# A projection in seven products of quarters, and work of VectorE handed to ScalarE, in a two-layer attention kernel

## The chip, the cores and the metric

The kernel runs on one core of a Trainium2 chip. The metric is device time in microseconds (us). Before the change three runs gave 2559.35, 2559.91 and 2560.78 us; their median, 2559.91 us, is the time that the change is measured against. One further execution, taken by the hardware profiler, gives the durations below; it took 2559.32 us.

Short names: PE is TensorE, and PEld its loading of weights; DVE is VectorE; ACT is ScalarE; POOL is GpSimd; SP is the engine that issues most transfers.

## The reference

The input x is 8 images of 512 channels by 32 x 32 points, so 1024 tokens. Two attention layers follow each other; all is float32.

```
# layer 0, for each of 8 images; 8 heads of 64 channels
h   = group_norm(x)
qkv = qkv_w @ h + qkv_b
q, k, v = fake_quant(q), fake_quant(k), fake_quant(v)    # 255 levels over the whole tensor
w   = softmax((q*s)^T (k*s));   a = w applied to v
x   = x + proj_w @ a + proj_b                            # "the projection"
# layer 1: one head of 512 channels
h   = group_norm(x)
q, k, v = wq h, wk h, wv h
x   = x + wp @ (softmax(q k^T / sqrt(512)) v)
```

`fake_quant` rounds x/scale, adds a zero point, clips to 0..255 and scales back. Its scale needs the minimum and the maximum over all images, so layer 0's q, k and v are computed for all images before its attention starts.

## The kernel before, in words

**Two phases.** Phase one computes layer 0's q, k and v of all images and stores them in HBM. Phase two interleaves, on all engines, the attention of layer 0 for image b+1 with layer 1 of image b, and ends with layer 1 of the last image alone.

**Attention of layer 0** (`attention`, L1018) is a generator. Its unit is one pair of heads, 512 query tokens and 128 keys; there are 512 units, and one `advance()` runs four. A unit takes: `scores` (two PE matmuls `st` into a PSUM pair, and ACT's exponential `pt<-st`); `split`, which writes `pt` as two float16 parts, the first by a cast on ACT or POOL (`two<-pt`), the second by a subtraction on DVE (`two<-pt,two`, a "sum" in the code, 128 x 1024); `over_keys` (PE matmuls `av`, which need both parts); and `totals` (PE matmuls `sm`). There are four `pt` buffers: the exponential of unit u needs the subtraction of unit u-4 (`need`, L1048). There are two PSUM pairs for `st`. In a dense step the scores of units u+6 and u+7 come first; in a late step, the one after a projection, `over_keys` of two units comes first, then the scores, then `over_keys` of the other two.

**Quantizing.** `load_pair` (L961) fetches the next pair's q, k and v; for each, `quant` (L890: times 1/scale, plus a magic number that rounds) works in place on 128 x 1024, and `quant2` (L893) clips and converts. Both are on DVE: 12 of each per image.

**Layer 1's big products** go by `seven` (L1393): a 512 x 512 product is cut into quarters and made from seven products of quarters instead of eight, with sums of quarters prepared on DVE. Two PSUM banks take turns, so product i+2 waits until product i has been read out. **The projection** (`project`, L1296) is plain: for each half of the tokens and each of four blocks of output channels, four matmuls 128 x 512; DVE then adds bias and residual in one instruction (`h<-pj,vec,h`), stores the result, and takes statistics (`gst_b<-h`) for layer 1's norm. The projection of image b+1 stands inside layer 1 of image b, in `o_run` after its fourth product (`first`, L1764): an attention step, half 0, an attention step (dense), half 1, an attention step (late), and the rest of `o_run`, into which the norm's steps (`norm1`, L1344) are placed. `norm1` normalizes the first half of the tokens at once (four DVE instructions 128 x 512) and leaves the second half as chores.

**What sets the order.** Each engine executes in program order. That order is written by a planner (`InOrder`, L72) with three clocks, `pe.t`, `dve.t` and `act.t`. A matmul moves `pe.t` by 1.677 ns per column of float32 (L213); DVE work on n elements costs `elements(n)`. `do` places work now. `later` puts work among an engine's chores with a time when its inputs are ready and a due time. Before each `do`, `fill` takes chores that fit into the gap, earliest start first, then earliest due. `settle(name)` places all chores of that name now, and `need` does so for subtractions.

```python
return 0.21 + n * 0.957e-3                 # elements(n), L159
ready = pe.t + 0.25 if ready is None else ready          # do
self.fill(ready)
self.t = max(self.t, ready) + cost
if begin + cost > limit + 0.15:            # fill, L138: does not fit, stays a chore
    continue
```

The names used below: `wp` is the projection's weights, `x_d` the HBM copy of its result, `h` (in the code `xts[b]`) the tile with the residual and then the normed input, `ao` layer 0's attention output, `gps_b` the two small matmuls of the norm, `g` the first product of layer 1.

Of the kernel before, what the change touches and what calls it, by code (L numbers as in the profile page):

```python
# [9 lines left out]
F32 = mybir.dt.float32  # L10
# [48 lines left out]
def attn_pair_kernel(  # L59
# [166 lines left out]


    def norm_steps(
        src, dst, wcol, bank, nm, ccs=range(CC), fine=False, put=None, mv=None, apply=None
    ):  # L230

        n, c0 = len(ccs), ccs[0]
        put = put or (lambda hf, cost, work: work())
        if mv is None:
            st, mv = stat_tiles(n, nm)
            for i, cc in enumerate(ccs):
                for hf in range(NH):
                    dve.bn_stats(st[:, i, hf, :], src(cc, hf))  # L240
                aggregate(mv, st, i)
                if fine and i + 1 < n:
                    yield
        yield
        ps = bank(f"gps_{nm}")[:, 0:n]
        mm(ps, lhsT=gavg, rhs=mv[:, :, 0], start=True, stop=True)

        d = small.tile([P, n], F32, tag=f"gd{n}", name=f"gd_{nm}")
        mean = small.tile([P, n], F32, tag=f"gmean{n}", name=f"gmean_{nm}")

        def offsets():
            dve.tensor_sub(d, mv[:, :, 0], ps)
            dve.tensor_copy(mean, ps)
            dve.tensor_mul(d, d, d)
            dve.tensor_add(d, d, mv[:, :, 1])

        dve.do(0.6, offsets)
        yield
        ps2 = bank(f"gps2_{nm}")[:, 0:n]
        mm(ps2, lhsT=gavg, rhs=d, start=True, stop=True)  # L260
        rstd = small.tile([P, n], F32, tag=f"grstd{n}", name=f"grstd_{nm}")
        dve.do(0.15, lambda: dve.tensor_scalar(rstd, ps2, EPS, None, ALU.add))
        nc.gpsimd.tensor_tensor(rstd, rstd, mhalf[:, 0:n], ALU.pow)
        dve.do(
            0.15, lambda: dve.tensor_mul(rstd, rstd, vec[:, wcol + c0 : wcol + c0 + n]), dve.t + 1.4
        )
        if apply is not None:
            off = small.tile([P, n], F32, tag=f"goff{n}", name=f"goff_{nm}")
            dve.scalar_tensor_tensor(off, mean, -1.0, rstd, ALU.mult, ALU.mult)
            for i, cc in enumerate(ccs):  # L270
                apply(cc, rstd[:, i : i + 1], off[:, i : i + 1])
                yield
            return
        for hf in range(NH):
            for i, cc in enumerate(ccs):
                put(hf, 0.5, lambda i=i, cc=cc, hf=hf: dve.tensor_scalar(
                    dst(cc, hf), src(cc, hf), mean[:, i : i + 1], rstd[:, i : i + 1],
                    ALU.subtract, ALU.mult,
                ))
                if fine and i % 2 == 1:  # L280
                    yield
        if not fine:
            yield
# [23 lines left out]
    with ExitStack() as fast:  # L307
# [579 lines left out]

        kept_u = l2p.tile([P, 3, 2, 256], F32, name="kept_u")

        def quant(raw, dst, i):  # L890
            dve.tensor_scalar(raw, raw, rcp[:, i : i + 1], MAGIC, ALU.mult, ALU.add)

        def quant2(raw, dst, i):  # L893
            dve.tensor_scalar(dst, raw, bhi[:, i : i + 1], MAGIC, ALU.min, ALU.subtract)
# [66 lines left out]
        def load_pair(b, j, u=None):  # L961

            nm = f"{b}_{j}"
            raws = []

            def fetch(i, src):
                if (b, j, i) == (0, 0, 2):
                    raw = aop.tile([P, NH, 512], F32, tag="ao", name="raw_first").rearrange(
                        "p h n -> p (h n)"
                    )  # L970
                else:
                    raw = raw_p.tile([P, T], F32, tag="raw", name=f"raw_{nm}_{i}")
                nc.sync.dma_start(
                    raw if i < 2 else raw.rearrange("p (t d) -> p t d", t=NT), src
                )
                raws.append(raw)

            def whole(raw, _, i):
                quant2(raw.rearrange("p (t d) -> p t d", t=NT)[:, 3::4, :], vfs[j], i)

            fetch(0, q_d[b][j])
            fetch(1, k_d[b][j])
            qt = qkp.tile([P, T], BF, tag="q", name=f"q_{nm}")
            kt = qkp.tile([P, T], BF, tag="k", name=f"k_{nm}")
            vt = qkp.tile([P, NT, P], F16, tag="v", name=f"v_{nm}")
            todo = (qt, kt, vt.rearrange("p t d -> p (t d)"))

            if b == 0:
                vfs[j] = xp.tile([P, 2, 256], F32, tag="x", name=f"vf_{nm}")[:, :, 0:P]

            def quants(i):
                for n, step in enumerate((quant, quant2, *([whole] if i == 2 and b == 0 else []))):
                    name, work = "qk" if i < 2 else "qv", lambda step=step: step(raws[i], todo[i], i)
                    if u is None or InOrder.planned:
                        dve.later(name, 0.7, work, pe.t + 12.0, 45.0)
                    else:
                        at = u + (7, 9, 15)[i] + n + (8 if b and j else 0)
                        dealt.append((at, name, work))
                        if (i, n) == (0, 1):
                            dealt.append((at, "qk", fetch_v))  # L1000

            def fetch_v():
                if len(raws) == 2:
                    fetch(2, v_d[b][:, :, bass.ts(j, P)])
                quants(2)

            if (b, j) == (0, 0):
                fetch(2, v_d[b][:, :, bass.ts(j, P)])
            quants(0)
            quants(1)  # L1010
            if u is None or InOrder.planned:
                dve.later("qk", 0.0, fetch_v)
            return qt, kt, vt
# [4 lines left out]
        def attention():  # L1018
# [138 lines left out]
            def finish(b, j, hf, u):  # L1157
# [26 lines left out]

                def divide():
                    dve.scalar_tensor_tensor(aot, aot, scl[:, 2:3], rs, ALU.mult, ALU.mult)

                def spread():
                    r = rcs[:, n * 16 : (n + 1) * 16]
# [74 lines left out]
                dma(xts[b][:, :, bass.ts(hf, 512)], x_v[b, :, :, bass.ts(hf, 512)])  # L1264

        def load_wp(b, dma):
            wps[b] = l2p.tile([P, CC, C], F32, tag="sums", name=f"wp0_{b}")
            dma(wps[b], w_sq[WP0])

        def load_first(u):  # L1270

# [21 lines left out]
            for t, src in zip(wm_tiles(b), wm_d):  # L1293
                act.dma_start(t, src)

        def project(b, bank=bank):  # L1296

            settle("ao")  # L1300
            st, mvs[b] = stat_tiles(CC, f"b{b}")
            wp0 = wps.pop(b)
            for hf in range(NH):
# [40 lines left out]
        def norm1(b, bank=bank):  # L1344
# [3 lines left out]

            def put(hf, cost, work):
                if hf == 0:  # L1350
                    dve.do(cost, work)
                else:
                    dve.later("h", cost, work, within=27.0)

            def put_sum(hf, i, work):
                if hf == 0:
                    dve.later("t4" if i == 3 else "t", elements(512), work, within=10.0 + 2.0 * i)
                else:
                    put(hf, elements(512), work)

            for n, _ in enumerate(norm_steps(
                at, at, V_GN1W, bank, f"b{b}", put=put, mv=mvs[b]
            )):
                if n == 2:
                    sums[b] = l2p.tile(
                        [P, 3, NH, CC // 2, 256], F32, tag="sums", name=f"sums2_{b}"
                    )
# [22 lines left out]
            dve.later("o", 0.25, spread, pe.t + 4.0, 5.0)  # L1390
            return rs

        def seven(nm, pairs, keep, whole, add, bank=bank):  # L1393

            nonlocal turn
            turn ^= 1  # L1400
            x, y = (bank(f"{nm}_{i}").rearrange("p (t n) -> p t n", t=2) for i in range(2))

            def product(n, ps, start):
                left, right = pairs[n]
                k = left.shape[1]
                for t in range(2):
                    for i in range(k):
                        mm(
                            ps[:, t, :], lhsT=left[:, i, bass.ts(t, P)], rhs=right[:, i, :],
                            start=start and t == 0 and i == 0, stop=(i == k - 1),  # L1410
                            skip_group_check=True,
                        )
# [4 lines left out]
                (5, x, False, whole, None),  # L1417
            )
            for i, (n, ps, start, out, m) in enumerate(work):
                awaits(free[(i + turn) % 2])  # L1420
                product(n, ps, start)
                free[(i + turn) % 2] = out(ps) if m is None else out(m, ps)
                yield i + 1

        free = [0.0, 0.0]
        turn = 0

        def slots(gq):
# [226 lines left out]
        def layer1(b, steps):  # L1655
# [46 lines left out]
            for hf in range(NH):  # L1702
# [52 lines left out]
                if last and b + 1 < B:  # L1755
                    load_wp(b + 1, act.dma_start)
                    load_x2(b + 1, act.dma_start)
                if done >= B:
                    load_x1(b, hf, 0, 1, rx, aop)
                settle("v")  # L1760
                between = [lambda: iter((1,)), lambda: iter(()), lambda: iter(())]
                if b + 1 < B and last:

                    def first():  # L1764
                        nonlocal ahead
                        yield -1
                        yield from project(b + 1, score_bank)
                        yield 2
                        ahead = norm1(b + 1, score_bank)
                        next(ahead)  # L1770
# [534 lines left out]
```

## Time and profile before

| what | us |
|---|---|
| median of three runs | 2559.91 |
| the profiled execution, by the device | 2559.32 |
| its span, first to last instruction | 2557.2 |
| from one image to the next in phase two (the same instruction, 907.76 and 1148.06) | 240.3 |
| PE idle in 940 to 1180, by the profile | 1.2 |

How to read the lines. A group's row has the line, engine, operation, output<-inputs, shapes and count, then busy time and mean duration in ns, then the idle time in front. L91 is the planner's own helper, so groups are told apart by tiles. A float32 matmul leaves two records, so half of image b's projection (16 matmuls) shows as 32. The ends of PE records are modelled; the step from start to start is what PE really takes. A timeline row has start, duration, engine, what it does, how many merged instructions, and in brackets the idle time before and what ended it.

### The profile page before, as it was taken

How to read it: one execution, taken by the hardware profiler on the slowest of the kernel's cores; microseconds unless marked ns; L12 is line 12 of the kernel's file. 1: busy time of each engine (PE TensorE's matmuls, PEld its weight loads, DVE VectorE, ACT ScalarE, POOL GpSimd, SP SyncE). 2: the span in 40 equal slices, each digit the busy share in tenths (PEclk: the TensorE clock that was granted, in tenths of full speed). 3: DMA queues.
4: the chain of work that ended last, by engine and by line, in shares of the span. 5: the costliest groups of instructions: out<-in, count | busy, mean ns of one | idle time of the engine just before them, and what ended most of it. 6: DMA issues, size and time to landing. Idle time of an engine off the chain costs nothing.

```text
span 2557.2 us, 38727 instructions
## 1 busy us (share of the span) xinstructions
PE 2515.9 (98%) x15670; PEld 1746.2 (68%) x15670; DVE 1897.6 (74%) x2747; ACT 1346.5 (53%) x1685; POOL 186.0 (7%) x167
## 2 busy tenths in 40 slices
PE   8999999999999999999999999999999999999998
PEld 4788888873357756775777577667756775777787
DVE  7887776668887778777877787777778777885544
ACT  3332223319857655665666466656655665664121
POOL 0000000001100001000100100010101000100000
PEclk9999999999999999999999999999999999999999
DMA  4533333236622232223313222322232123212211
GB/s 168 177 142 125 131 124 122 109 131 162 162 88 63 79 116 85 58 74 122 98 57 100 92 79 78 110 92 63 79 112 88 55 71 128 96 42 80 87 38 39
DMA packets 160717, 250.70 MB, mean 98 GB/s; under 512 B 27152, under 2 KB 93712, under 8 KB 159120
## 3 DMA queue, kind: packets, MB, share of 16 engines
q1 hardware_dynamic: 125792, 182.81, 21.6%
q10 hardware_dynamic: 30560, 57.71, 6.5%
q0 software_dynamic: 4176, 7.60, 1.7%
q8 instruction: 125, 2.05, 0.3%
q14 instruction: 64, 0.52, 0.1%
HBM read 153.64 MB, written 86.28 MB: 94 GB/s over the span
## 4 chain that ended last, share of the span: by engine, by line
PE 85%; DVE 5%; ACT 2%; issue 1%; DMA 1%; POOL 0%; SPq 0%; ACTq 0%; DVEq 0%
PE s L209 15%; PE o L209 13%; PE qkps L209 12%; PE pj L209 8%; PE av L209 8%; PE v2ps L209 7%; PE vps L209 6%; PE g L209 6%; PE st L209 4%; PE sm L209 3%; DVE two L91 2%; ACT pt L91 1%; PE fold L209 1%; DVE h L91 1%; DVE acc L91 0%
## 5 line engine op out<-in xcount | busy, mean ns | idle before, releaser
L91 ACT ACTIVATE pt<-st,esc 128x1024 f32<-128x1024 f32 x467 | 496.4, 1114 | 332.1 <-PE st L209 317.6
L91 DVE TENSOR_TENSOR two<-pt,two 128x1024 f16<-128x1024 f32 x467 | 561.5, 1216 | 131.0 <-POOL two L1092 100.7
L91 ACT CAST two<-pt 128x1024 f16<-128x1024 f32 x346 | 350.8, 1055 | 6.9 <-ACT p L91 5.1
L1092 POOL CAST two<-pt 128x1024 f16<-128x1024 f32 x112 | 146.0, 1304 | 1409.4 <-PE sm L209 746.3
L209 PE MATMUL av<-two,v 128*32 128x512 f16 x3968 | 245.9, 381 | 2.5 <-DVE two L91 2.1
L209 PE MATMUL s<-g,h 128*128 128x256 f32 x1024 | 233.4, 380 | 0.0
L209 PE MATMUL pj<-ao,wp 128*128 128x512 f32 x512 | 224.1, 595 | 0.6 <-DVE h L91 0.6
L209 PEld LDWEIGHTS s<-g,h 128*128 128x128 f32 x1024 | 192.9, 190 | 31.0 <-issue 4.3
L91 ACT ACTIVATE u_ring<-qkps,qkbt 128x512 f32<-128x512 f32 x89 | 60.9, 685 | 243.8 <-PE qkps L209 219.3
L209 PEld LDWEIGHTS <-v 128*32 128x32 f16 x3968 | 91.8, 96 | 140.0 <-issue 66.7
L209 PEld LDWEIGHTS pj<-ao,wp 128*128 128x128 f32 x512 | 96.0, 190 | 122.5 <-issue 110.8
L209 PE MATMUL s<-g,sums 128*128 128x256 f32 x768 | 178.4, 381 | 0.2 <-DVE p L91 0.2
L209 PE MATMUL o<-p,v 128*128 128x256 f32 x768 | 175.2, 382 | 1.0 <-DVE p L91 1.0
L209 PE MATMUL st<-q,k 64*128 64x512 bf16 x1024 | 163.4, 382 | 11.9 <-ACT pt L91 7.5
L209 PEld LDWEIGHTS o<-p,v 128*128 128x128 f32 x768 | 144.3, 190 | 27.1 <-issue 5.7
L209 PEld LDWEIGHTS s<-g,sums 128*128 128x128 f32 x768 | 144.7, 190 | 24.2 <-issue 4.6
L209 PE MATMUL sm<-two,ones 128*32 128x512 f16 x1984 | 136.0, 379 | 0.0
L209 PEld LDWEIGHTS <-k 64*128 64x128 bf16 x1024 | 34.8, 94 | 143.8 <-issue 142.2
L209 PE MATMUL qkps<-half,w_high 128*128 128x512 f32 x480 | 132.4, 398 | 0.0
L209 PE MATMUL qkps<-half,w_mix 128*128 128x512 f32 x480 | 130.6, 394 | 1.0 <-DVE half L91 1.0
L209 PE MATMUL qkps<-half,w_low 128*128 128x512 f32 x480 | 130.5, 394 | 0.0
L209 PE MATMUL v2ps<-wm,h 128*128 128x256 f32 x512 | 119.9, 383 | 1.9 <-ACT g L91 1.3
(226 smaller groups left out, 3902.2 us busy)
## 6 DMA issues: line engine op xcount, KB each, us to landing
rs<-rs_d SPq DMA_DIRECT2D x76, 256.0 KB
x<-in_x_dram SPq DMA_DIRECT2D x32, 512.0 KB
q_d<-wa SPq DMA_DIRECT2D x32, 512.0 KB
k_d<-wa SPq DMA_DIRECT2D x32, 512.0 KB
v_d<-v_ring SPq DMA_DIRECT2D x32, 512.0 KB
raw<-q_d SPq DMA_DIRECT2D x32, 512.0 KB
raw<-k_d SPq DMA_DIRECT2D x32, 512.0 KB
x_d<-h SPq DMA_DIRECT2D x64, 256.0 KB
```

The costliest lines, as they stand in the source:

```text
L91: ins = self.latest = op(*args, **kw).ins
L209: ins = nc.tensor.matmul(ps, lhsT=lhsT, rhs=rhs, **kw).ins
L1092: copy(two[:, 0], pt)
```

## The change

1. **The projection of images 1 to 7** (`project_seven`, new) goes by `seven`. Image 0 keeps the plain form and prepares the sums of the weights' quarters once (`combine_wp`), which go to HBM; `load_wp` then loads 1.5 MB per image in three transfers, where it loaded 1 MB in one, and a fourth weight sum (256 KB) is fetched at the start of each projection.
2. Its read-outs are all on DVE and add into the residual in place: seven per half, 128 x 512. Sums of quarters of `ao` are made on DVE: two 128 x 512 beforehand (`first_sums`), two at the start (`second`), and in each half four 128 x 256 between the first products. The two PSUM banks are the halves of one PSUM pair. Statistics follow after the sixth and seventh product of a half, two at each.
3. **The bias** is added to the residual by ACT, four 128 x 1024 chores per image (`add_bias`), settled when the projection starts.
4. **The norm** of layer 1 is applied by ACT instead of DVE, eight 128 x 512 per image (`scaled`); one small DVE instruction is added for the offset.
5. **Quantizing's first step**, wherever the planner's clocks are on (the later images), goes to ACT (`shift`); the second, on DVE, first settles the first.

```diff
+        if scaled:
+            off = small.tile([P, n], F32, tag=f"goff{n}", name=f"goff_{nm}")
+            dve.do(0.15, lambda: dve.scalar_tensor_tensor(
+                off, mean, -1.0, rstd, ALU.mult, ALU.mult
+            ))
...
+                if scaled:
+                    put(hf, 0.6, lambda i=i, cc=cc, hf=hf: act.activation(
+                        dst(cc, hf), src(cc, hf), AF.Identity, bias=off[:, i : i + 1],
+                        scale=rstd[:, i : i + 1],
+                    ))
...
+        def shift(raw, dst, i):
+            act.activation(raw, raw, AF.Identity, bias=magic, scale=rcp[:, i : i + 1])
...
-                    if u is None or InOrder.planned:
-                        dve.later(name, 0.7, work, pe.t + 12.0, 45.0)
+                    if InOrder.planned and n == 0:
+                        act.later(name, 1.02, lambda: shift(raws[i], todo[i], i), pe.t + 12.0, 35.0)
+                    elif u is None or InOrder.planned:
+
+                        def rest(work=work):
+                            if InOrder.planned:
+                                act.settle(name)
+                            work()
+
+                        dve.later(name, 0.7, rest, pe.t + 13.2, 45.0)
...
+                    if b and j == 1:
+                        first_sums(b)
...
-            wps[b] = l2p.tile([P, CC, C], F32, tag="sums", name=f"wp0_{b}")
-            dma(wps[b], w_sq[WP0])
+            wps[b] = w = l2p.tile([P, 6, CC // 2, C // 2], F32, tag="sums", name=f"wp0_{b}")
+            dma(w[:, 0:2].rearrange("p i k n -> p (i k) n"), w_sq[WP0][:, :, 0 : C // 2])
+            dma(w[:, 2], w_sq[WP0][:, CC // 2 :, C // 2 :])
+            dma(w[:, 3:6], wp_d[:, 0:3])
...
+        def add_bias(b):
+            for cc in range(CC):
+                act.later("xb", 1.05, lambda cc=cc: act.activation(
+                    xts[b][:, cc, :], xts[b][:, cc, :], AF.Identity,
+                    bias=vec[:, V_PB0 + cc : V_PB0 + cc + 1],
+                ), pe.t + 17.0, 24.0)
...
+        def project_seven(b, room):
+
+            settle("at")
             settle("ao")
+            act.settle("xb")
...
+            act.dma_start(s4, wp_d[:, 3])
...
+            for k in range(2):
+                dve.do(elements(512), lambda k=k: second(k))
...
+                def into(q, row, col, full, hf=hf):
+
+                    def add(ps):
+                        there = dve.do(elements(512), lambda: tt(q, ps, q, ALU.add))
+                        if full is not None:
+                            nc.sync.dma_start(x1_d[b][row][hf][:, :, col * 256 : (col + 1) * 256], q)
+                        return there
...
+                for step in seven(
+                    f"pj_{b}_{hf}",
+                    ((a11, h11), (a12, h21), (s2, th), (s3, h11), (s1, t1), (s4, h22), (a22, h21)),
+                    lambda n, ps: keeps[n](ps), into(q12, 0, 1, 1), lambda n, ps: adds[n](ps),
+                    lambda _: next(banks), True,
+                ):
+                    if step in (1, 2):
+                        for k in range(2):
+                            h = (h11, h21)[step - 1][k]
+                            args = (h, th[k], h) if step == 1 else (h, h, th[k])
+                            dve.do(elements(256), lambda args=args: tt(*args, ALU.subtract))
+                    for oc in {6: (2, 3), 7: (0, 1)}.get(step, ()):
+                        dve.later("pj", 0.62 + 0.2 * hf, lambda oc=oc, stats=stats: stats(oc), within=4.0)
+                    chore()
+                if hf + 1 < NH:
+                    yield -1
+            settle("pj")
...
             def put(hf, cost, work):
                 if hf == 0:
-                    dve.do(cost, work)
+                    act.do(cost, work, dve.t + 0.1)
                 else:
-                    dve.later("h", cost, work, within=27.0)
+                    act.later("h", cost, work, within=22.0)
...
-                        yield from project(b + 1, score_bank)
+                        yield from project(b + 1, vt)
```

More of the change, by code (lines that the diff above doesn't have):

```diff
@@ L228, in norm_steps @@
     def norm_steps(
-        src, dst, wcol, bank, nm, ccs=range(CC), fine=False, put=None, mv=None, apply=None
+        src, dst, wcol, bank, nm, ccs=range(CC), fine=False, put=None, mv=None, apply=None,
+        scaled=False,
     ):
@@ L273, in norm_steps @@
             return
+        if scaled:
[3 more added lines that the diff above has]
+            ))
         for hf in range(NH):
             for i, cc in enumerate(ccs):
[L276 to L279, printed above, removed]
+                if scaled:
[3 more added lines that the diff above has]
+                    ))
+                else:
+                    put(hf, 0.5, lambda i=i, cc=cc, hf=hf: dve.tensor_scalar(
+                        dst(cc, hf), src(cc, hf), mean[:, i : i + 1], rstd[:, i : i + 1],
+                        ALU.subtract, ALU.mult,
+                    ))
                 if fine and i % 2 == 1:
@@ L888, in attn_pair_kernel @@
         kept_u = l2p.tile([P, 3, 2, 256], F32, name="kept_u")
+        magic = const.tile([P, 1], F32, name="magic")
+        dve.memset(magic, MAGIC)
         def quant(raw, dst, i):
             dve.tensor_scalar(raw, raw, rcp[:, i : i + 1], MAGIC, ALU.mult, ALU.add)
+        def shift(raw, dst, i):
+            act.activation(raw, raw, AF.Identity, bias=magic, scale=rcp[:, i : i + 1])
         def quant2(raw, dst, i):
@@ L1294, in load_wm, with combine_wp @@
                 act.dma_start(t, src)
-        def project(b, bank=bank):
-            settle("ao")
+        wp_d = dram.tile([P, 4, CC // 2, C // 2], F32, tag="wp", name="wp_d")
+        def combine_wp():
+            wc = l2p.tile([P, 3, NT // 2, 256], F32, tag="vsum", name="wp_combined").rearrange(
+                "p a (s k) n -> p (a s) k n", k=2
+            )
+            a11, a12, a21, a22 = (
+                wps[0][:, k * CC // 2 : (k + 1) * CC // 2, m * 256 : (m + 1) * 256]
+                for m in range(2) for k in range(2)
+            )
+            s2, s3, s1, s4 = (wc[:, i] for i in range(4))
+            for args in (
+                (s1, a21, a22, ALU.add), (s2, s1, a11, ALU.subtract),
+                (s3, a11, a21, ALU.subtract), (s4, a12, s2, ALU.subtract),
+            ):
+                dve.later("wc", elements(512), lambda args=args: tt(*args), within=20.0)
+            dve.later("wc", 0.0, lambda: nc.sync.dma_start(wp_d, wc[:, 0:4]), within=20.0)
@@ new lines, in add_bias, with first_sums @@
+        def add_bias(b):
[4 more added lines that the diff above has]
+                ), pe.t + 17.0, 24.0)
+        def first_sums(b):
+            for cc in range(CC // 2):
+                h = ao[b, cc]
+                dve.later("at", elements(512), lambda h=h: tt(
+                    h[:, :, 256:512], h[:, :, 256:512], h[:, :, 0:256], ALU.subtract
+                ), within=30.0)
@@ new lines, in project_seven, with second, stats @@
+        def project_seven(b, room):
+            settle("at")
+            settle("ao")
+            act.settle("xb")
+            st, mvs[b] = stat_tiles(CC, f"b{b}")
+            w = wps.pop(b)
+            a11, a12, a22, s2, s3, s1 = (w[:, i] for i in range(6))
+            t2 = room[:, 0 : NT // 2, 0:256].rearrange("p (k h) n -> p k h n", h=NH)
+            s4 = room[:, NT // 2 : NT // 2 + 2, 0:256]
+            act.dma_start(s4, wp_d[:, 3])
+            left, right = slice(0, 256), slice(256, 512)
+            def second(k):
+                tt(t2[:, k], ao[b, 2 + k][:, :, right], ao[b, k][:, :, right], ALU.subtract)
+            for k in range(2):
+                dve.do(elements(512), lambda k=k: second(k))
+            for hf in range(NH):
+                h11, t1, h21, h22 = (
+                    [ao[b, c + k][:, hf, n] for k in range(2)] for c in (0, 2) for n in (left, right)
+                )
+                th = [t2[:, k, hf] for k in range(2)]
+                q11, q12, q21, q22 = quarters(b, hf)
+                at = pair_ps(f"pj_{b}_{hf}")
+                banks = iter((at[:, 0, :], at[:, 1, :]))
+                def into(q, row, col, full, hf=hf):
[4 more added lines that the diff above has]
+                        return there
+                    return add
+                def stats(oc, hf=hf):
+                    dve.bn_stats(st[:, oc, hf, :], xts[b][:, oc, bass.ts(hf, 512)])
+                    if hf == NH - 1:
+                        aggregate(mvs[b], st, oc)
+                keeps = [into(q, *at_, None) for q, at_ in ((q11, (0, 0)), (q21, (1, 0)), (q22, (1, 1)))]
+                adds = [into(q, *at_, 1) for q, at_ in ((q11, (0, 0)), (q21, (1, 0)), (q22, (1, 1)))]
+                for step in seven(
[3 more added lines that the diff above has]
+                    lambda _: next(banks), True,
+                ):
+                    if step in (1, 2):
[9 more added lines that the diff above has]
+            settle("pj")
+            for k in [k for k in ao if k[0] == b]:
+                del ao[k]
@@ L1301, in project @@
+        def project(b, room=None):
+            if b:
+                yield from project_seven(b, room)
+                return
+            settle("ao")
+            combine_wp()
             st, mvs[b] = stat_tiles(CC, f"b{b}")
@@ L1350, in put, with sum_up @@
                 if hf == 0:
-                    dve.do(cost, work)
+                    act.do(cost, work, dve.t + 0.1)
                 else:
-                    dve.later("h", cost, work, within=27.0)
+                    act.later("h", cost, work, within=22.0)
             def put_sum(hf, i, work):
+                def sum_up():
+                    act.settle("h")
+                    work()
                 if hf == 0:
-                    dve.later("t4" if i == 3 else "t", elements(512), work, within=10.0 + 2.0 * i)
+                    dve.later(
+                        "t4" if i == 3 else "t", elements(512), work, act.t + 0.1, 10.0 + 2.0 * i
+                    )
                 else:
-                    put(hf, elements(512), work)
+                    dve.later("h", elements(512), sum_up, within=27.0)
             for n, _ in enumerate(norm_steps(
-                at, at, V_GN1W, bank, f"b{b}", put=put, mv=mvs[b]
+                at, at, V_GN1W, bank, f"b{b}", put=put, mv=mvs[b], scaled=True
             )):
                 if n == 2:
+                    if b == 0:
+                        settle("wc")
                     sums[b] = l2p.tile(
@@ L1391, in inverse1, with seven @@
             return rs
-        def seven(nm, pairs, keep, whole, add, bank=bank):
+        def seven(nm, pairs, keep, whole, add, bank=bank, alone=False):
             nonlocal turn
-            turn ^= 1
+            turn ^= not alone
+            free, side = ([0.0, 0.0], 0) if alone else (busy, turn)
             x, y = (bank(f"{nm}_{i}").rearrange("p (t n) -> p t n", t=2) for i in range(2))
@@ L1408, in product @@
                         mm(
-                            ps[:, t, :], lhsT=left[:, i, bass.ts(t, P)], rhs=right[:, i, :],
+                            ps[:, t, :], lhsT=left[:, i, bass.ts(t, P)],
+                            rhs=right[i] if type(right) is list else right[:, i, :],
                             start=start and t == 0 and i == 0, stop=(i == k - 1),
@@ L1419, in seven @@
             for i, (n, ps, start, out, m) in enumerate(work):
-                awaits(free[(i + turn) % 2])
+                if not alone:
+                    side = turn
+                awaits(free[(i + side) % 2])
                 product(n, ps, start)
-                free[(i + turn) % 2] = out(ps) if m is None else out(m, ps)
+                free[(i + side) % 2] = out(ps) if m is None else out(m, ps)
                 yield i + 1
-        free = [0.0, 0.0]
+        busy = [0.0, 0.0]
         turn = 0
@@ L1757, in layer1 @@
                     load_x2(b + 1, act.dma_start)
+                    add_bias(b + 1)
                 if done >= B:
```

## The prediction, made before the changed kernel was run

> **What bounds the kernel now.** I read the page's first part, then the stages, then the order of time around one projection.
>
> ```profile
> PE 2515.9 (98%) x15670; PEld 1746.2 (68%) x15670; DVE 1897.6 (74%) x2747; ACT 1346.5 (53%) x1685; POOL 186.0 (7%) x167
> ```
>
> PE is busy throughout. The stages' columns are: stretch, length, then busy us of PE, PEld, DVE, ACT, POOL.
>
> ```profile
> 940.00:1180.00 240.00, 238.80 (x1652) 161.57 (x1652) 182.55 (x232) 151.40 (x188) 23.26 (x17) 1.00 0.27 85
> ...
> 930.70:944.60 13.90, 13.90 (x36) 6.00 (x32) 11.45 (x16) 4.04 (x6) 0.00 (x0) 1.00 0.52 170
> 944.60:949.20 4.60, 4.08 (x57) 1.42 (x56) 3.44 (x5) 3.59 (x4) 1.28 (x1) 1.00 0.22 79
> 949.20:963.00 13.80, 13.80 (x36) 6.00 (x32) 8.81 (x13) 3.47 (x4) 0.00 (x0) 1.00 0.24 89
> ```
>
> One image takes 240.3 us and PE waits 1.2 of them: only less PE work can gain, and every new wait of PE costs its full length. DVE is the second engine, and inside the first half of the projection it is already busy 11.45 of 13.90 us. So the question is what DVE still owes when PE leaves the projection. In order of time (image 2's projection, later rows its norm):
>
> ```profile
> 930.72 14.00 PE L209 MATMUL pj<-ao,wp 128*128 128x512 f32 x32
> ...
> 949.24 14.00 PE L209 MATMUL pj<-ao,wp 128*128 128x512 f32 x32
> ...
> 958.05 1.17 DVE L91 TENSOR_TENSOR two<-pt,two 128x1024 f16<-128x1024 f32 x1
> ...
> 960.51 1.22 DVE L91 TENSOR_TENSOR two<-pt,two 128x1024 f16<-128x1024 f32 x1
> ...
> 963.17 1.05 PE L209 MATMUL av<-two,v 128*32 128x512 f16 x16
> 963.28 0.75 DVE L91 SCALAR_TENSOR_TENSOR h<-pj,vec,h 128x512 f32<-128x512 f32 x1 [0.71 <-PE pj L209]
> 964.06 0.69 DVE L91 BATCH_NORM_STATS2 gst_b<-h 128x6 f32<-128x512 f32 x1
> ...
> 965.13 1.04 PE L209 MATMUL av<-two,v 128*32 128x512 f16 x16
> ...
> 977.91 1.91 DVE L91 TENSOR_SCALAR h<-h,gmean_b,grstd_b 128x512 f32<-128x512 f32 x4
> 978.09 0.61 PE L209 MATMUL st<-q,k 64*128 64x512 bf16 x4
> 978.52 2.12 ACT L91 ACTIVATE pt<-st,esc 128x1024 f32<-128x1024 f32 x2 [5.64 <-PE st L209]
> ...
> 981.33 0.61 PE L209 MATMUL st<-q,k 64*128 64x512 bf16 x4
> ...
> 981.86 3.72 PE L209 MATMUL g<-h,wa 128*128 128x256 f32 x16
> ```
>
> To be seen: the attention's subtractions (`two<-pt,two`) fall between two read-outs of the projection, so that the `av` at 965.13, 2.0 us after the step's start, finds them done.
>
> **PE's saving.** Half a projection takes 930.72 to 944.65, 13.93 us. The same form of product as the new one is `g`: 16 records (two products) from 981.86 to the next product at 985.42, 3.56 us with a start of 0.1, so 0.2165 per record. Seven products are 56 records: 12.1, with the start 12.2. Saved: 1.71 per half, 3.42 per image, 23.9 for seven images. [...] An image's projection goes from 64 to 112 records of weight loads at 0.19[...]. The row decides: `g` has a load of 0.19 inside each step of 0.2165 and still keeps that pace. I count nothing.
>
> **DVE in total.** Per image it loses eight read-outs (8 x 0.75 = 6.0), eight norms (35.4/64 = 0.55 each, 4.4) and twelve `raw<-raw,rcp` (10.5), 20.9. It gains fourteen read-outs like `p<-s,kept_u` (14 x 0.69 = 9.7), four sums of 512 (2.8) and eight of 256 (0.44 each, half of a pair `x<-kept_u,ob,x` of 0.87; 3.5), 16.0. So 5 us less of 183. This relief gains nothing of itself, since PE hardly waited.
>
> **DVE inside the halves** is another matter. The planner takes 4 x 256 x 1.677 ns = 1.717 us per product and elements(512) = 0.700 per read-out. Between two read-outs 1.017 stay free, with the 0.15 that `fill` allows 1.167. A subtraction costs elements(1024) = 1.190: it misses by 0.023 us, and so is placed in no gap of either half. Smaller chores (`quant2` 0.7, scalings 0.7 and 0.91, statistics 0.62 or 0.82) fit. Before, the gap was 3.435 - 0.74. (These figures are the program's own and give the order; the durations below are the trace's.)
>
> Half 0: subtraction u+6 still precedes it; u+7, u+8 and u+9 stay, with three of four statistics. Let PE end at T. The last read-out ends at T+0.95, the subtractions at 2.15, 3.35 and 4.5. The dense step's `av` need only u+7 late in the step, but the exponential of u+11 waits for u+7, ends at 3.35, and holds the PSUM pair of the fourth `st`, which starts at about 3.4 instead of 2.95. **Cost 0.5.**
>
> Half 1: the three old statistics go first (about 1.8 us) into the gap before its first read-out; they leave 1.1, again under 1.19, so u+10 isn't placed there either. At the end T' there stand: the last read-out to T'+0.95, three statistics with aggregates at 0.9 (`settle("pj")` puts them first) to 3.65, subtractions u+10 and u+11 to 6.0, u+12 and u+13 behind. The late step's second `av` needs u+10 and u+11: it starts at T'+6.0 instead of T'+2.1. Behind it in PE's queue stand the rest of the step and all of `o_run`. **Cost 3.9.** Bounds for both together: 1.5 (if two subtractions find room after all) to 6.
>
> **The norm on ACT.** Nearest row: ACT with pointers for scale and bias on the same shape,
>
> ```profile
> L91 ACT ACTIVATE x<-x,goff,rstd x7: 798/813/814, 10.4 to 27.5; 128x512 f32<-128x512 f32 x7
> ```
>
> and two in 1.52 us, so 0.71 apart. Four take 2.9 where DVE took 1.91, and they stand on ACT in front of the two exponentials at 978.52. Those shift to about 980.9; the third and fourth `st` wait for the PSUM pairs until 982.0 and 983.0 instead of 981.33 and 981.6, and `g` behind them starts at 983.2 instead of 981.86. **Cost 1.3**; bounds 0 (the exponentials have slack that I don't see) and 2.4 (all of the shift). [...] 1.234 (`x<-x,goff_a,grstd_a`, 128 x 1024) less 0.87, some 4.4 us per image. By the rows they cost PE nothing, as ACT is busy 151 of 240 us and would be at about 176: they are chores with 20 us of room. [...] For the shifts I take 0; bounds -0.5 and 1.5 per image, if they delay exponentials, or if `quant2`, which waits on DVE for a shift still queued on ACT, holds subtractions up.
>
> **Bias on ACT.** One of the four is placed before the exponentials; three follow them, 1.14 each, from 931.9 to 935.3. The first read-out needs the second of them (933.1, against 932.65 without): 0.5 us later, within DVE's 0.7 of slack. Casts behind them move by 3.4 us, which the wait for the subtractions hides. Cost 0; up to 1 if that cover is gone.
>
> **Transfers.** The residual and 1 MB of weights, asked for at 907.8, come at 357 to 380 GB/s and are in by about 920; 0.5 MB more is 1.4 us, before ACT's first bias at about 924. The fourth weight sum, issued after the biases at 935.3, has until 941. On SP the stores keep their number. All hidden: 0; up to 1 if the sum is late.
>
> **Sum.** Images 1 to 6: -3.4 + 0.5 + 3.9 + 1.3 = +2.3 each, +13.8. Image 7 has no attention beside it: -3.4, +0.35 for the bias in front of its first read-outs, +0.3 for the norm, so -2.8. Image 0: four sums of 0.69 beside PE, +0.5 (0 to 2). Total +11.5 on the profiled execution's 2559.3 (its span 2557.2 and 2.1 around it): 2570.8; on the median 0.6 more, rounded to 2571.
>
> **Rivals.**
> - *The subtractions find room.* Place: the gaps of 1.167 us in the halves. Price: most of the 3.9 us, and half of the 0.5. It decides from 0.023 us more per gap, or if two more go between the halves. For: DVE has 5 us less per image, and in the trace it really idles in such gaps. Against: the order is fixed by the planner's clocks. Then -3.4 + 0.3 + 0.5 + 1.3 = -1.3 x 6, -2.8, +0.5: -10, 2550; with a hidden norm 2542; at best 2536.
> - *Half of it*: only u+10 finds room; 1.2 us less per image, 2564, about the old time.
> - *ACT becomes the bound*: biases, shifts and norms delay exponentials and the seven-products' copies in other stages too, 2 us per image more: 2585. For: real shifts take 1.14 to 1.23, the planner says 1.02. Against: 89 us of ACT idle per image.
>
> **Chances.** Subtractions in the way 0.60, half of it 0.14, room for them 0.19, ACT 0.07. A measurement tells 0.2%, 5 us, from no change. Slower by more: 0.66 (the first and last case, less 0.04 whose time ends within, and 0.03 of the half case); within: 0.15; faster: 0.19. The likeliest case's own range is 2562 to 2582. The range for 8 in 10, with a part of the faster case and the start of the ACT case, is 2548 to 2584.
>
> **What would show it.** Right: `av<-two,v` waits for DVE `two` some 4 us after each of six projections, PE records of `pj` at 0.2165, four ACT `h<-h` ahead of exponentials with `st` waiting for `pt`; the image's period 242 to 243 us. Wrong: a period under 240, DVE subtractions between read-outs of `pj`, or PE waiting inside a half for read-outs.

## The result, and the profile after

The changed kernel takes 2736.6 us (2735.6 to 2739.3), 1.069 times the time before (95% interval 1.067 to 1.071): 177 us more than the 2559.9 before, where 11 were predicted. The sign was right and the size far off.

The page's first part, then PE's waits in the whole run (us in total, times, longest):

```profile
PE 2554.4 (93%) x16006; PEld 1820.5 (67%) x16006; DVE 1878.8 (69%) x2743; ACT 1510.6 (55%) x1856; POOL 176.6 (6%) x167
```

```profile
PE pj L209 <- DVE h L91: 71.1, 85, 3.9
PE st L209 <- ACT pt L91: 35.2, 41, 4.0
PE av L209 <- DVE two L91: 22.5, 21, 2.0
```

PE is busy 93% instead of 98%. Before, `st<-ACT pt` was 7.5 us, `av<-DVE two` 2.1, and the first wait, of the projection for its own read-outs, was 0.6. The stretches, as before: the 240 us, and half 0.

```profile
940.00:1180.00 240.00, 221.91 (x1554) 155.99 (x1547) 163.82 (x214) 158.06 (x192) 20.66 (x16) 0.98 0.23 72
943.70:962.60 18.90, 13.89 (x62) 10.06 (x58) 9.58 (x18) 8.26 (x10) 0.00 (x0) 1.00 0.43 139
```

They show image 1, whose projection starts at 943.70 (the prediction's rows, which it calls image 2's, are image 1's too). PE's idle time in the 240 us has gone from 1.2 to 18.1, and a half takes 18.9 and 18.6 instead of 13.93; I had expected 12.2. In order of time, PE and DVE inside half 0:

```profile
949.49 1.99 PE L209 MATMUL pj<-v,wp 128*128 128x256 f32 x8 [0.78 <-DVE h L91]
951.59 0.69 DVE L91 TENSOR_TENSOR h<-pj,h 128x512 f32<-128x512 f32 x1 [1.49 <-PE pj L209]
...
952.34 1.99 PE L209 MATMUL pj<-ao,wp 128*128 128x256 f32 x8 [0.85 <-DVE h L91]
```

PE and DVE take turns. A product starts some 2.8 us after the last one (2.85 here, mostly 2.78), and only when the read-out of the product just before it has ended; the two banks were there so that it need wait only for the one before that. Next the late step, which starts at 986.11:

```profile
989.27 6.55 DVE L91 TENSOR_TENSOR two<-pt,two 128x1024 f16<-128x1024 f32 x5
990.49 0.62 PE L209 MATMUL av<-two,v 128*32 128x512 f16 x8 [2.04 <-DVE two L91]
991.63 0.62 PE L209 MATMUL av<-two,v 128*32 128x512 f16 x4 [0.52 <-DVE two L91]
...
993.99 4.12 PE L209 MATMUL o<-g,vsum 128*128 128x256 f32 x16
```

The whole step, before and after:

```profile
963.17:967.08 3.91, 3.91 (x58) 1.41 (x57) 1.90 (x4) 2.24 (x3) 1.04 (x1) 1.00 0.18 67
986.11:993.99 7.88, 5.32 (x57) 1.43 (x56) 7.67 (x11) 2.49 (x3) 1.90 (x1) 0.84 0.10 34
```

Five subtractions stand behind the statistics, and the step lasts 7.88 us, to the start of `o` at 993.99, instead of 3.91. PE waits 2.56 of it, and its own work takes 5.32 instead of 3.91, because the granted clock, the third column from the right, falls in the middle of the step (0.84 in the mean). Then the norm:

```profile
1005.01 0.81 ACT L91 ACTIVATE h<-h,goff_b,grstd_b 128x512 f32<-128x512 f32 x1 [5.30 <-DVE goff_b L91]
...
1005.73 5.03 ACT L91 ACTIVATE h<-h,goff_b,grstd_b 128x512 f32<-128x512 f32 x7
...
1011.81 0.56 PE L209 MATMUL st<-q,k 64*128 64x512 bf16 x2 [3.10 <-ACT pt L91]
...
1013.35 6.36 PE L209 MATMUL g<-h,wa 128*128 128x256 f32 x16
```

One and seven norms, so all eight of the image, stand in front of the exponentials. And `g`, which took 3.56 us before, takes 6.2 (to the next product at 1019.55). Two stretches tell why, again by the granted clock.

```profile
992.00:993.00 1.00, 1.00 (x12) 0.18 (x4) 1.00 (x2) 0.80 (x1) 1.00 (x1) 0.50 0.00 0
1016.00:1018.00 2.00, 2.00 (x6) 1.57 (x5) 2.00 (x4) 0.83 (x3) 0.00 (x0) 0.50 0.00 0
```

PE idles in 988.5 to 990.5 and in 1008.7 to 1011.8. About 0.9 us after the first of these stretches and 0.1 after the second, the granted clock falls to exactly half, where it stays for about 3.4 us the first time and 6.8 the second; `g` runs nearly all of its time at half clock.

The next image's late step has the same two waits, 2.04 and 0.52, but there the clock stays up:

```profile
1250.66:1257.73 7.07, 4.44 (x57) 1.42 (x57) 6.86 (x11) 2.53 (x3) 1.47 (x1) 1.00 0.12 40
```

So the waits, without the clock, make the step 3.2 us longer, and the lower clock makes it 0.8 more. The clock fell there in images 1, 3 and 5 and not in 2, 4 and 6; behind the norm it fell in all six.

The last stage is o_run's first attention step, before the projection:

```profile
918.84 1.23 ACTq L91 DMA_DIRECT2D wp<-in_w_sq_dram  x2
...
920.62 1.03 ACTq L91 DMA_DIRECT2D h<-in_x_dram  x2
...
923.77 1.04 ACT L91 CAST two<-pt 128x1024 f16<-128x1024 f32 x1
...
924.87 0.40 PE L209 MATMUL av<-two,v 128*32 128x512 f16 x4 [0.68 <-ACT two L91]
```

ACT spends 918.84 to 921.65 on issuing transfers, so the cast that `av` needs is late (0.68), and so is the subtraction that needs the cast (another 0.86 for the next four). The planner counts 0.5 us of ACT for each issue, which fits that the cast now stands behind an exponential that it preceded in the kernel before. An image takes 264.2 us (the six from the weights' load at 920.1 to the last one at 2505.4), 23.9 more than before. Stage by stage, for image 1, from start to start:

| stage | before | after | difference |
|---|---|---|---|
| first attention step | | | +1.9 |
| half 0, half 1 | 13.93, 13.93 | 18.9, 18.6 | +9.6 |
| dense step | 4.59 | 4.91 | +0.3 |
| late step, and `o` behind it | 3.91, 3.56 | 7.88, 3.96 | +4.4 |
| norm: from the first `st` to `g` | 3.77 | 7.95 | +4.2 |
| `g` at half clock | 3.56 | 6.2 | +2.6 |
| `v2ps` waiting for `g` on ACT | | | +1.2 |

They come to 24.2, within 0.3 of the whole.

### The profile page after: what moved, and what is told of

Its sections match the earlier page's. It is cut to its first block, busy times and chain, and to the rows that moved or that the text cites. A ratio compares the mean times of both kernels' runs of the same rounds, so it can differ in the third digit from the quotient of the medians.

```text
span 2733.6 us, 39719 instructions
## 1 busy us (share of the span) xinstructions
PE 2554.4 (93%) x16006; PEld 1820.5 (67%) x16006; DVE 1878.8 (69%) x2743; ACT 1510.6 (55%) x1856; POOL 176.6 (6%) x167
## 4 chain that ended last, share of the span: by engine, by line
PE 75%; DVE 9%; ACT 6%; issue 3%; DMA 2%; POOL 1%; ACTq 0%; SPq 0%; DVEq 0%; POOLq 0%
PE s L209 14%; PE o L209 12%; PE qkps L209 11%; PE pj L209 7%; PE v2ps L209 7%; PE vps L209 6%; PE g L209 6%; PE av L209 5%; PE st L209 3%; PE sm L209 3%; DVE h L91 3%; DVE two L91 3%; ACT pt L91 2%; ACT h L91 1%; ACT raw L91 1%
## 5 line engine op out<-in xcount | busy, mean ns | idle before, releaser
L91 DVE TENSOR_TENSOR two<-pt,two 128x1024 f16<-128x1024 f32 x467 | 569.4, 1241 | 164.7 <-POOL two L1118 97.1
L209 PE MATMUL av<-two,v 128*32 128x512 f16 x3968 | 253.5, 385 | 27.1 <-DVE two L91 22.5
L1118 POOL CAST two<-pt 128x1024 f16<-128x1024 f32 x112 | 136.7, 1220 | 1574.1 <-ACT pt L91 881.9
L209 PE MATMUL pj<-ao,wp 128*128 128x256 f32 (+1 forms) x624 | 169.2, 416 | 49.1 <-DVE h L91 49.1
L209 PE MATMUL st<-q,k 64*128 64x512 bf16 x1024 | 170.6, 390 | 43.0 <-ACT pt L91 35.2
L209 PEld LDWEIGHTS pj<-ao,wp 128*128 128x128 f32 x624 | 113.8, 191 | 103.6 <-DVE h L91 72.4
L91 DVE TENSOR_TENSOR h<-pj,h 128x512 f32<-128x512 f32 x98 | 67.8, 691 | 137.1 <-PE pj L209 128.4
L209 PEld LDWEIGHTS s<-g,sums 128*128 128x128 f32 x768 | 144.7, 190 | 24.2 <-issue 4.6
L209 PE MATMUL g<-h,wa 128*128 128x256 f32 x512 | 137.2, 422 | 4.0 <-ACT h L91 2.7
```

What stands on the lines that cost most here:

```text
L91: ins = self.latest = op(*args, **kw).ins
L209: ins = nc.tensor.matmul(ps, lhsT=lhsT, rhs=rhs, **kw).ins
L1118: copy(two[:, 0], pt)
```

## The experiments

Each run shared its chip with the kernel before, at 2559.5 to 2559.7 us there. Theory A throughout: four separate causes (the shared pair, the norm's queue, late subtractions, transfers and shifts on ACT). The rivals are with each run.

**1. Two PSUM pairs instead of one**, all else as after.

```diff
-                at = pair_ps(f"pj_{b}_{hf}")
-                banks = iter((at[:, 0, :], at[:, 1, :]))
+                banks = iter([score_bank(f"pj_{b}_{hf}_{i}") for i in range(2)])
```

> The changed kernel with the projection's two PSUM banks taken from two PSUM pairs instead of the two halves of one. Theory A (PE may not write one half of a pair while DVE's read-out of the other half is outstanding, so each product waits for the read-out just before it): a half of the projection goes from 18.9 and 18.6 us to 12.2 to 13, some 12 us per image and 85 in all, so about 2650 us; the waits of pj for DVE h fall from 71 us to under 10. Rival B (PE waits for operands that DVE changes in place, the residual or the sums of ao, not for the bank): the spacing of 2.78 us per product stays and the time stays at 2736.

Measured: 2647.7 us (2646.3 to 2649.4), ratio 1.035 (1.033 to 1.036), 89 us less than after, 12.7 per image. Half 0 in this run:

```profile
943.61:955.89 12.28, 12.28 (x60) 10.55 (x57) 9.58 (x18) 8.25 (x10) 0.00 (x0) 1.00 0.60 190
```

PE is busy all through, and the half lasts the 12.2 us that I had worked out; in the whole run PE's waits for the projection's read-outs fall from 71.1 to 2.5 us. Operands that DVE changes in place, the rival, are the same in both runs and so are not the cause. So the pace of products was right, and the wait came of putting both banks into one tile. That the wait is the program's, which may count a tile as one thing, and not the memory's, is my reading and not shown: the runs show only that a second tile removes it.

**2. The norm back on DVE**, all else as after.

```diff
-                    act.do(cost, work, dve.t + 0.1)
+                    dve.do(cost, work)
...
-                    act.later("h", cost, work, within=22.0)
+                    dve.later("h", cost, work, within=27.0)
...
```

> The changed kernel with layer 1's norm back on DVE. Theory A (eight norms stand on ACT ahead of two exponentials, PE idles over 3 us and then runs g at half clock; 4.2 + 2.6 + up to 1.2 us per image for six images): 2688 to 2696 us, granted clock back to about 0.99. Rival B (the low clock comes from the wait after the projection, and only the exponentials' shift goes): about 2711.

Measured: 2680.4 us (2677.8 to 2683.1), ratio 1.047 (1.046 to 1.049): 56 us less than after, 8 us more than A had at most. `st<-ACT pt` falls from 35.2 to 9.9 us, the mean granted clock rises from 0.986 to 0.995; `av<-DVE two` stays, 22.1. Two waits change places: `v2ps<-ACT g` falls from 8.1 to 2.4, and `v2ps<-DVE v`, which after doesn't have, comes in with 4.2. Run 4 shows where that one comes from.

**3. The weights in one transfer**, all else as after; the quarters lie in HBM in the order in which they are used.

```diff
-            dma(w[:, 0:2].rearrange("p i k n -> p (i k) n"), w_sq[WP0][:, :, 0 : C // 2])
-            dma(w[:, 2], w_sq[WP0][:, CC // 2 :, C // 2 :])
-            dma(w[:, 3:6], wp_d[:, 0:3])
+            dma(w, wp_d[:, 0:6])
...
```

> The changed kernel with all quarters of the projection's weights kept together in HBM, so that one transfer of 1.5 MB takes the place of three on ACT's queue. Theory A (the two more issues on ACT push a cast behind two exponentials, and av waits for it, 1.9 us per image in o_run's first attention step): about 2724 us. Rival B (the cast is late for another reason): 2736, and the bytes alone, which are the same, show nothing.

Measured: 2723.5 us (2721.7 to 2726.2), ratio 1.064 (1.062 to 1.066): 13 us less, 1.9 per image, as the trace had it. The cast stands before the exponentials again (at 920.58). The bytes are the same: it was the issuing on ACT's queue that cost, not the transfer. Whether by its own time or by the order that the planner made of it, this run doesn't separate.

**4. Quantizing's first step on ACT, alone**, in the kernel before.

> The kernel before with nothing but quantizing's first step on ACT. Theory A (the shifts are chores in ACT's idle time): 2558 to 2562 us. Rival B (they delay exponentials and evictions, 0.5 to 1.5 us per image): 2563 to 2570.

Measured: 2575.2 us (2573.6 to 2577.2), ratio 1.006 (1.005 to 1.008): 15.7 us more, above both theories. In order of time around `v2ps` of one image:

```profile
1262.11 1.24 ACT L91 ACTIVATE raw<-raw,magic,rcp 128x1024 f32<-128x1024 f32 x1
...
1263.38 0.75 DVE L91 TENSOR_SCALAR v<-raw,bhi 128x1024 f16<-128x1024 f32 x1 [1.64 <-ACT raw L91]
1264.05 0.68 DVE L91 TENSOR_TENSOR v<-v2ps,kept_u 128x512 f32<-128x512 f32 x1
...
1264.79 1.99 PE L209 MATMUL v2ps<-wm,sums 128*128 128x256 f32 x8 [0.69 <-DVE v L91]
```

The shift was settled, placed at the last moment, when its second step's turn came on DVE. DVE stands 1.64 us before it; a read-out is queued behind, and PE waits for that. Run 9 tests this.

**5. The projection alone**: after, with the edits of 1 to 3 and quantizing back on DVE; the bias stays on ACT.

> The projection in seven products alone: two PSUM pairs, one transfer for the weights, the norm and quantizing back on DVE; the bias stays on ACT. Theory A (what is left of the loss is the subtractions that stand behind the statistics after the second half): the saving of 24 us against 4 us in the late step and 0.3 in the dense one for six images, and the clock lowered by that wait; about 2562 us, 2555 to 2570, with av waiting for DVE two some 20 us in all. Rival B (the subtractions no longer stand in the way once the pair is gone): 2537 to 2545.

Measured: 2567.4 us (2566.3 to 2568.9), ratio 1.003 (1.002 to 1.004). The late step of the same projection:

```profile
964.81 0.76 PE L209 MATMUL av<-two,v 128*32 128x512 f16 x8 [2.04 <-DVE two L91]
...
968.31 5.51 PE L209 MATMUL o<-g,vsum 128*128 128x256 f32 x16
```

```profile
968.00:974.00 6.00, 6.00 (x21) 4.76 (x20) 2.27 (x3) 6.00 (x7) 0.00 (x0) 0.67 0.18 51
```

The same 2.04 us wait stands in a kernel from which all other causes are gone, and here the lowered clock reaches into `o` (0.67 in the mean of 968 to 974). The late step of this image lasts 7.89 us instead of 3.91. The saved matmuls are given back entirely.

**6. The subtractions put into the halves**: run 5, with one pending subtraction placed after each of the steps 3 to 6 of a half, whatever the planner makes of the gap.

```diff
+                    if step in (3, 4, 5, 6):
+                        i = next((i for i, c in enumerate(dve.chores) if c[0] == "sum"), None)
+                        if i is not None and dve.chores[i][3] <= dve.t:
+                            dve.begin(i)
                     chore()
```

> The same, and after the third to the sixth product of each half one pending subtraction of the attention is placed at once, though it doesn't fit the planner's gap (1.190 against 1.167 us). Theory A: av no longer waits for DVE two after the projection, read-outs slip by up to 0.5 us inside their 0.7 of slack; 2536 to 2545 us, faster than the kernel before. Rival B (the read-outs slip more and PE waits inside the halves instead): 2555 to 2570.

Measured: 2538.9 us (2536.7 to 2540.2), ratio 0.992 (0.990 to 0.994), 0.8% faster than before and 28.5 us better than run 5. In half 1:

```profile
952.27 1.22 DVE L91 TENSOR_TENSOR two<-pt,two 128x1024 f16<-128x1024 f32 x1
953.41 0.69 DVE L91 TENSOR_TENSOR h<-pj,h 128x512 f32<-128x512 f32 x1
954.01 1.22 DVE L91 TENSOR_TENSOR two<-pt,two 128x1024 f16<-128x1024 f32 x1
```

The stretches are half 1 and the late step:

```profile
946.20:958.47 12.27, 12.27 (x62) 10.54 (x58) 9.81 (x15) 3.41 (x4) 0.00 (x0) 1.00 0.18 61
958.47:962.37 3.90, 3.90 (x57) 1.41 (x56) 3.66 (x9) 2.24 (x3) 1.04 (x1) 1.00 0.39 134
```

Three subtractions stand between read-outs in this half (two are shown), and PE is busy throughout both stretches; the gaps that the planner found 0.023 us too short hold them on the chip. The late step is 3.90 again. An image takes 236.88 us instead of 240.3: the 3.42 of the prediction's first step, to the digit. So nothing else of the new projection (the bias on ACT, the sums of quarters, 0.5 MB more) costs an image anything once these waits are gone. In all the run gains 20.8 us, 3 less than seven images at 3.42; where those are lost is open.

**7. The norm on ACT, alone**, in the kernel before.

> The kernel before with nothing but layer 1's norm on ACT. Theory A (all eight norms stand ahead of two exponentials whatever the projection does, PE waits about 4 us and runs the first product of g at half clock): 6 to 7 us per image for seven images, 2600 to 2608 us. Rival B (only the four norms of the first half stand there, the other four came ahead because the late projection had delayed the subtractions, and the low clock came from two waits close together): 1.3 us per image as predicted, about 2569.

Measured: 2620.3 us (2619.4 to 2621.2), ratio 1.024 (1.023 to 1.026), 60.6 us more, over A's size too. Here too one and seven norms precede the exponentials, PE waits 3.31 us, and then:

```profile
998.00:1004.00 6.00, 6.00 (x19) 4.90 (x20) 5.96 (x9) 3.59 (x6) 0.32 (x1) 0.65 0.04 15
```

An image takes 6.8 to 7.6 us more; image 0 takes 11.9 more up to the next image's norm, with a wait of 3.9 for a copy of `wm` that stands behind the norms on ACT.

**8. Only the first half's four norms on ACT**, the kernel before otherwise; the second half's stay chores of DVE.

> The kernel before, with only the first half's four norms on ScalarE; the second half's four stay VectorE chores. Theory A: the price of the norm is a queue. With the norm on ScalarE alone eight instructions (5.8 us) stood ahead of the exponentials, PE waited 3.3 + 0.4 us for them and the next product ran at about half clock. Four instructions (2.9 us where DVE took 1.9) leave a wait of 1.0 to 1.3[...]: 1.3 us per image as in my prediction, 2569 us (2564 to 2577), granted clock near 0.999. Rival B: any ScalarE norm in front of the exponentials costs its whole length[...]: 4 to 6 us per image, 2590 to 2605, clock under 0.995.

Measured: 2576.5 us (2575.5 to 2578.0), ratio 1.007 (1.006 to 1.008).

```profile
983.16 0.81 ACT L91 ACTIVATE h<-h,goff_b,grstd_b 128x512 f32<-128x512 f32 x1 [5.04 <-DVE goff_b L91]
...
983.88 2.21 ACT L91 ACTIVATE h<-h,goff_b,grstd_b 128x512 f32<-128x512 f32 x3
...
987.14 0.39 PE L209 MATMUL st<-q,k 64*128 64x512 bf16 x2 [0.50 <-ACT pt L91]
```

```profile
987.00:990.00 3.00, 2.26 (x11) 1.58 (x11) 2.90 (x4) 3.00 (x4) 1.25 (x1) 1.00 0.00 0
```

From the norm's first small product (`gps_b`) to `g` it is 1.35 us more than before in the images 1 and 2: the 1.3 that I had predicted for four. With waits of 0.5 and 0.6 the clock stays at 1.00. The rest of the 17 us is mostly image 0's, 5.75 us more in which the 3.9 us wait for `wm` stands again. So A holds, B doesn't.

**9. The second step of quantizing later**: run 4, with 8 us instead of 1.2 between the steps' ready times.

```diff
-                        dve.later(name, 0.7, rest, pe.t + 13.2, 45.0)
+                        dve.later(name, 0.7, rest, pe.t + 20.0, 45.0)
```

> The kernel before with quantizing's first step on ScalarE, as in the run of that change alone (2575.2), but the second step becomes ready at pe.t + 20.0 instead of 13.2, so that ScalarE has 8 us instead of 1.2 to have done the first. Theory A: those 2.1 us per image came from VectorE standing in front of a shift that was settled at that very moment, with read-outs that PE needs queued behind. Then most of it goes: 2560 to 2566. Rival B: the twelve shifts delay exponentials and copies on ScalarE, whenever they are done: it stays at 2572 to 2578.

Measured: 2564.2 us (2561.9 to 2566.4), ratio 1.002 (1.001 to 1.003). Of run 4's 15.7 us 4.7 are left, and `v2ps<-DVE v` (4.2 us there) has left the list of waits: most of it was the standing before a shift, not the work on ACT. The 4.7 are not explained.

**Do the parts add up?** After less 89 (run 1), 56 (run 2), 13 (run 3) and 15.7 (run 4) is 2562.9; run 5, all of it at once, has 2567.4. Nearly independent, then; 4.5 us stay unassigned. One of the four is borrowed: the shifts were measured in the kernel before, and in the changed kernel `v2ps<-DVE v` isn't among the waits. What they cost there no run shows.

## Why the prediction was wrong, step by step

- **"Seven products are 56 records: 12.1, with the start 12.2"**: the pace was right (12.28 and 12.27 in runs 1 and 6), but that PE would reach it failed. I took it that product i+2 waits for the read-out of product i, as in `seven` before, and read over the line of the diff by which both banks are one tile. Each product waited for the one just before: 2.78 us instead of 1.73, 12.7 us per image and 89 in all, half of the 177. My list of what would prove me wrong had "PE waiting inside a half for read-outs", but no rival had a price for it.
- **The norm on ACT, 1.3**: the price per norm was right (run 8: 1.35). The count was wrong. The second half's four were chores on DVE, and I left them aside; on ACT the planner finds room for them before the exponentials, so eight stood there. With the wait of 3.1 to 4.0 us the granted clock went to 0.50, which I had nowhere: 2.6 more in image 1. In all 56 to 61 us (runs 2 and 7) instead of some 8.
- **The late step, 3.9**: the mechanism was right, with `two` behind the statistics and `av` waiting at the place named; run 5 shows it alone, run 6 takes it away. That image 1 has 3.97 (7.88 less 3.91) is in part luck: the waits are worth 3.2 (7.07 less 3.91 in images 2, 4 and 6), and 0.8 come from the clock, which I had put at nothing. It also costs 0.4 in `o` behind the step, and 1.8 in the image shown of run 5. **The dense step, 0.5**: 0.3.
- **Transfers, "all hidden: 0"**: wrong by 1.9 per image (run 3). I counted bytes and landing times; the cost was the issuing, which pushed the cast behind the exponentials.
- **The shifts, 0, bounds -0.5 to 1.5**: alone, in the kernel before, they cost 2.2 per image, outside the bounds. The way (`quant2` waits on DVE for a shift still queued on ACT) was named, but what it holds up was a read-out, not subtractions.
- **The bias, 0**: nothing in run 6 speaks against it.
- **The rivals**: room for the subtractions was indeed worth that much, but by hand (run 6), not by the planner. ACT becoming the bound was the nearest in kind, yet its 2 us per image were a sixth of what ACT's queue cost (8.0 for the norm, 1.9 for issuing, 2.2 for the shifts).

## What to carry to other kernels

Before counting on two banks, look whether they are two tiles: whoever waits may wait for the tile (89 us here, run 1). A chore moved to another engine stands wherever that engine's planner finds room, so count all of them, its DMA issues too, in front of the next thing that PE needs. And when a planner refuses a gap by hundredths of a microsecond, place the work by hand and measure.

## What the runs showed of the hardware

The same wait was not always followed by the same clock. After the 2.04 us in the late step, with 0.52 close behind, the granted clock went to 0.50 in three of the changed kernel's six images (1, 3 and 5) and stayed at 1.00 in the other three; what decides between them is not shown. It stayed at 0.50 for 3.4 us each time. With the norm's waits it went to 0.50 in all six images, for 6.8 us: the wait is 3.10 in images 1, 3 and 5, and 3.95 to 3.97 in 2, 4 and 6, where the clock fell before the wait had ended. Behind image 0's norm a wait of 1.21 us was followed by 3.4 us at 0.50.

Six short waits did not lower it: in half 0 after the change PE idles 5.0 of 18.9 us, 0.8 to 1.0 at a time, at a granted clock of 1.00. Nor did the 0.50 and 0.61 us of run 8, also at 1.00. In image 1 the norm's wait of 3.10 us and the 2.6 that `g` then lost make 5.7, nearly twice the wait.
